# A soft mixture-of-experts stage: four places for the dispatch weights, its slot matrix loaded by block, and a later place for the second chunk's matmuls

## The chip, the cores and the metric

The kernel runs on one core of a Trainium2 chip. A core has a matrix engine (TensorE, PE in the profile; its weight loads are listed as PEld), a vector engine (VectorE, DVE), a scalar engine (ScalarE, ACT), a general engine (GpSimd, POOL) and a sync engine (SyncE, SP) that here issues the DMA transfers. Each engine works through its own queue of instructions in order and waits on semaphores where it needs another's result. The metric is the device time of one execution in microseconds (us).

## The reference

The reference is a sandwich of four layers on an input of 16 batch elements, 256 tokens and 128 features in float32. Every one of its eight sublayers computes `x = x + layernorm(sub(layernorm(x)))`: attention and a gated feed-forward in layer 0, linear and local attention and a soft mixture of experts in layer 1, attention and a feed-forward in layer 2, a state-space and attention trunk and an expert-choice mixture in layer 3. The change touches only the soft mixture of layer 1:

```python
def _L1_ffn_ref(x, phi, W, b):
    ...
    logits = jnp.einsum('bmd,dnp->bmnp', x, phi)
    dispatch = jax.nn.softmax(logits, axis=0)
    bsz, m, n, p = logits.shape
    combine = jax.nn.softmax(logits.reshape(bsz, m, n * p), axis=-1).reshape(bsz, m, n, p)
    slots = jnp.einsum('bmd,bmnp->bnpd', x, dispatch)
    y = jnp.einsum('bnpd,nde->bnpe', slots, W) + b[None, :, None, :]
    out = jnp.einsum('bnpd,bmnp->bmd', y, combine)
    return out
```

There are 64 experts (`n`) of 32 slots (`p`), so 2048 slots. The logits are normalised twice: over the 16 batch elements (`dispatch`, which mixes tokens into slots) and over the 2048 slots (`combine`, which mixes the experts' outputs back into tokens).

## The kernel before

One program computes all sublayers one after the other. The soft mixture is `stage_soft_moe` (line 1040). It works through the 2048 slots in 8 blocks of 256; a block has two chunks of 128 slots (4 experts each), and the 256 tokens are two tiles `t` of 128. The softmax over all slots is done with a running maximum: a block's outputs are added to `x` after the sum so far is faded by `exp(old maximum - new maximum)`.

Three generators do a block's work, and one iteration `n` of the loop at the end of the function runs them step by step side by side, for three blocks at once. Where a generator yields, the next one takes its step, so the source order of the steps is the order of priority; a scheduler then places the instructions into the engines' queues by that and by their dependences.

- `logits(n + 2)`: for each of the 16 batch elements two matmuls of the tokens with the block's 256 columns of `phi` into a PSUM bank `ps_s` (PE), a copy into `lg` (ScalarE, L1095) and a maximum into `mpart` (VectorE, L1096). Behind the last one come the running maximum `mtop` (L1100), its fade `mfade` (L1102, L1103) and `mless` (L1106).
- `slots(n + 1)`: `maxima(c, t)` for chunk c and tile t takes the maximum over the batch (VectorE, L1117 to L1120), subtracts it (L1121) and takes the exponential (ScalarE, L1122) in a tile `mdisp` of 8 KB per partition; `weights(c, t)` sums over the batch, takes the reciprocal and multiplies (VectorE, L1127 to L1134). `inputs(c, half)` multiplies tokens by these weights (PE, `ps_mm<-mdisp,mxn`) and ScalarE copies the result into `slT` (L1146); it needs both tiles' weights of the chunk. `experts(c, half)` adds the bias and multiplies by the expert's matrix `mw` (PE), and ScalarE copies into `my` (L1166). The expert matrices are loaded at the start of `slots` by SP.
- `share(n)`: for each batch element ScalarE takes the exponential of the logits (L1215), PE transposes it (`ps_t`, L1220), ScalarE copies the transpose into `meT` (L1222), PE multiplies with `my` (`ps_o`), VectorE adds into `x` (L1231; L1233 in the first block) and ScalarE takes the row sum into `mgot` (L1234). All its matmuls need the block's `my`, which is one buffer.

In the last block `share` starts an `end(g)` after every second batch element: the division by the sum of weights (L1249 to L1252), and for six of the eight groups a load of the stage's input back from DRAM into a tile of the name `slT` (SP, L1023) and the closing layer norm on VectorE and POOL (`soft_end`, up to L1037).

A tile name with a number of buffers is a ring of places: the next tile of that name waits until the readers of the oldest are done. `mdisp` has three places, `slT` three, `mw` two. PSUM is eight banks: two each for `mm`, `s`, `o` and `t`. `phi` is loaded whole (1024 KB) by one DMA near the program's start, with the stage's other weights, into a pool on the right side of the memory that is closed after this stage; work tiles lie on the left side. Behind the stage the program opens pools for the weights of layer 3 (`l_afc` and so on, `l3rows`) and starts layer 2's attention (`stage_l2_attn`), which begins with loads of its mask tables (`att_sel`, `att_rows`) through the same SP queue, casts of them on VectorE (`at_sel` L373, `b_rows` L375), and the reductions `at_nm` (L459).

Of the kernel before, what the change touches and what calls it, by code (L numbers as in the profile page):

```python
# [21 lines left out]
F32 = mybir.dt.float32  # L22
# [7 lines left out]
NB, SEQ, P, D = 16, 256, 128, 128  # L30
NG, NT, GT = 8, 4, 512
# [154 lines left out]
def idle(n):  # L186

    for _ in range(n):
        yield


def bc(ap, axis, n):

    ap = ap.unsqueeze(axis)
    shape = list(ap.shape)
    shape[axis] = n
    return ap.to_broadcast(shape)
# [842 lines left out]
def stage_soft_moe(k, x, w, wdram, bdram, xn, xs, fill):  # L1040
# [3 lines left out]

    nc, v = k.nc, k.nc.vector
    ident = k.c["ident"]
    phi = w["phi"]
    blocks, bs = 8, 2 * P
    sums = k.t([P, 2, NB], "sums", 1)
    xT = {}  # L1050
    tile_of = lambda b, t: (b // 2, 2 * (b % 2) + t)
# [3 lines left out]
    y = k.t([P, 2, NB, D + 1], "my", 1)  # L1055
# [4 lines left out]
    quarter = k.t([P, P], "mquarter", 1, dt=BF16)  # L1060
# [3 lines left out]
    def biases():  # L1064


        left = k.t([P, 16 * D], "mdisp", 3)
        nc.gpsimd.memset(left, 0.0)
        for i in range(3):
            nc.sync.dma_start(out=left[32 * i : 32 * i + 4, :], in_=bdram)  # L1070
        nc.gpsimd.tensor_copy(bias, left)
        for i in (1, 2):
            for at in (slice(32, 64), slice(64, P))[i - 1 :]:
                nc.gpsimd.tensor_tensor(left[at, :], left[at, :], bias[at, :], ALU.subtract)
                nc.gpsimd.tensor_copy(bias[at, :], left[at, :])

    def late(g):

        y = k.t([P, NT, D], "slT", 3)
        yield from k.norm_to(y, xn[g])  # L1080
        nc.gpsimd.tensor_tensor(x[g], x[g], y, ALU.add)
        yield
        yield from fill(g)

    def logits(n):
        lg = lgs[n % 2]
        part = k.t([P, 2, NB], "mpart", 2)
        for b in range(NB):
            if n == 0 and b % 2 == 0:
                xT[b // 2] = k.transposed(xn[b // 2], f"mxT{b // 2}", 1)  # L1090
            ps = k.ps("s").rearrange("p (t n) -> p t n", t=2)
            for t in range(2):
                g, at = tile_of(b, t)
                k.mm(ps[:, t, :], xT[g][:, at * P : (at + 1) * P], phi[:, n * bs : (n + 1) * bs])
            nc.scalar.copy(lg[:, :, b, :], ps)  # L1095
            v.tensor_reduce(part[:, :, b], ps, AX.X, ALU.max)  # L1096
            yield

        new = k.t([P, 2, NB], "mtop", 4)
        v.tensor_tensor(new, top[-1], part, ALU.max)  # L1100
        f = fade[n] = k.t([P, 2, NB], "mfade", 3)
        v.tensor_tensor(f, top[-1], new, ALU.subtract)  # L1102
        nc.scalar.activation(f, f, AF.Exp)  # L1103
        top.append(new)
        less[n] = k.t([P, 2, NB], "mless", 3)
        v.tensor_scalar(less[n], new, -1.0, None, ALU.mult)  # L1106

    def slots(n):

        lg = lgs[n % 2]  # L1110
        disp, rest = {}, []

        def maxima(c, t):
            src = lg[:, t, :, c * P : (c + 1) * P]
            e = disp[c, t] = k.t([P, NB, P], "mdisp", 3)
            m = k.t([P, P], "mm", 1)
            v.tensor_tensor(e[:, 0:8, :], src[:, 0:8, :], src[:, 8:16, :], ALU.max)  # L1117
            v.tensor_tensor(e[:, 0:4, :], e[:, 0:4, :], e[:, 4:8, :], ALU.max)
            v.tensor_tensor(e[:, 0:2, :], e[:, 0:2, :], e[:, 2:4, :], ALU.max)
            v.tensor_tensor(m, e[:, 0, :], e[:, 1, :], ALU.max)  # L1120
            v.tensor_tensor(e, src, bc(m, 1, NB), ALU.subtract)  # L1121
            nc.scalar.activation(e, e, AF.Exp)  # L1122

        def weights(c, t):
            e = disp[c, t]
            s = k.t([P, 4, P], "msum", 1)
            v.tensor_tensor(s, e[:, 0:4, :], e[:, 4:8, :], ALU.add)  # L1127
            for i in (8, 12):
                v.tensor_tensor(s, s, e[:, i : i + 4, :], ALU.add)
            for i in (2, 1):  # L1130
                v.tensor_tensor(s[:, 0:i, :], s[:, 0:i, :], s[:, i : 2 * i, :], ALU.add)
            r = k.t([P, P], "mrec", 1)
            v.reciprocal(r, s[:, 0, :])
            v.tensor_tensor(e, e, bc(r, 1, NB), ALU.mult)  # L1134

        def inputs(c, half):

            out = k.t([P, 8, P], "slT", 3)
            for q in range(2):
                ps = k.ps("mm").rearrange("p (b n) -> p b n", b=4)  # L1140
                for i in range(4):
                    b = 8 * half + 4 * q + i
                    for t in range(2):
                        g, at = tile_of(b, t)
                        k.mm(ps[:, i, :], xn[g][:, at, :], disp[c, t][:, b, :], t == 0, t == 1)
                nc.scalar.copy(out[:, 4 * q : 4 * q + 4, :], ps)  # L1146
            return out

        def experts(c, half, slT):

            pss = [k.ps("mm") for _ in range(2)]
            at = (2 * n + c) * D
            for ps in pss:
                k.mm(ps, quarter, bc(bias[:, at : at + D], 1, 4), True, False)
            for q, ps in enumerate(pss):
                for i in range(4):
                    for e in range(4):
                        k.mm(
                            ps[32 * e : 32 * e + 32, i * P : (i + 1) * P],
                            slT[:, 4 * q + i, 32 * e : 32 * e + 32],  # L1160
                            wc[c][:, e, :],
                            False,
                            True,
                        )
                b = 8 * half + 4 * q
                nc.scalar.copy(y[:, c, b : b + 4, 0:D], ps.rearrange("p (b n) -> p b n", b=4))  # L1166

        wc = []
        for c in range(2):
            at = 2 * n + c  # L1170
            wc.append(k.t([P, 4, D], "mw", 2))
            nc.sync.dma_start(out=wc[c].rearrange("p n d -> p (n d)"), in_=wdram[:, at * 512 : (at + 1) * 512])
        maxima(0, 0)
        yield
        maxima(0, 1)
        yield
        weights(0, 0)
        yield
        maxima(1, 0)
        yield  # L1180
        weights(0, 1)
        yield
        yield
        yield
        a = inputs(0, 0)
        yield
        b = inputs(0, 1)
        yield
        weights(1, 0)
        yield  # L1190
        maxima(1, 1)
        yield
        experts(0, 0, a)
        yield
        weights(1, 1)
        yield
        yield
        a = inputs(1, 0)
        yield
        experts(1, 0, a)  # L1200
        yield
        experts(0, 1, b)
        yield
        b = inputs(1, 1)
        yield
        experts(1, 1, b)

# [36 lines left out]
    def end(g, f, got):  # L1244


        bs = slice(2 * g, 2 * g + 2)
        r = k.t([P, 2, 2], "mend", 3)
        v.tensor_tensor(r, sums[:, :, bs], f[:, :, bs], ALU.mult)  # L1249
        v.tensor_tensor(r, r, got[:, :, bs], ALU.add)  # L1250
        rt = k.over[g] if g in k.over else k.t([P, NT], "mendt", 3)
        v.reciprocal(rt.rearrange("p (b t) -> p t b", b=2), r)  # L1252
        if g in k.over:
            return
        back = k.t([P, NT, D], "slT", 3)
        yield from soft_end(k, x[g], xs[:, g], rt, back)
        yield
        if g == 0:
            k.stats_nb(x[g], k.kept)
# [694 lines left out]
def program(ctx: ExitStack, tc: tile.TileContext, xin, dram, at, out):  # L1954
    nc = tc.nc
# [4 lines left out]
    def opened(name, side):  # L1960
        weights[name] = pool(name, side)
        return weights[name].__enter__()
# [4 lines left out]
    def load(p, name, only=None, dt=F32):  # L1967

        got = {}
        for n, (a, width) in at[name].items():  # L1970
            if only is not None and n not in only:
                continue
            src = dram[name][:, a : a + width]
            t = p.tile([src.shape[0], width], dt, tag=f"{name}_{n}", name=f"{name}_{n}")
            nc.sync.dma_start(out=t, in_=src)
            got[n] = t
        return got
# [20 lines left out]
    k = Ctx(tc, const, None, None)  # L1998
# [26 lines left out]
    closed("w0")  # L2025
    l2 = load(opened("wb", "right"), "l2")
    psoft = opened("soft", "right")
    l1f = load(psoft, "l1f")
    xs, xn, fill = soft_inputs(k, x, psoft)
    stage("l1a", "left", stage_l1_attn, l1, rows1, z, fill, xn, *hand, banks=RING_BANKS)  # L2030
    closed("z")
    closed("wa")

    stage("l1f", "left", stage_soft_moe, l1f, dram["l1fw"], dram["l1fb"], xn, xs, fill)
    closed("soft")
    pe = opened("we", "right")
# [50 lines left out]
```

## Time and profile before

Three runs took 2938.27, 2942.89 and 2943.25 us; their median is 2942.89.

| | us |
|---|---|
| median of three runs | 2942.89 |
| the profiled execution | 2940.6 |
| span of its profile | 2938.8 |
| the soft mixture in it | 931 to 1516.5 |
| mean granted clock of PE | 0.973 |

The profile is that of one execution. Its page begins with the busy time of each engine over the whole span; the trace behind it answers for any stretch of time. Four views are used below. The table by windows gives the busy time of each engine in a stretch. The timeline lists the instructions of one engine in order: start in us from the span's start, duration in us, engine, source line, operation, output tile, input tiles, shape, how many stand in the row, and in square brackets how long the engine had sat idle before it and on which engine's result it had waited. The DMA view gives size and time from issue to landing of each transfer, and the list of waits sums the idle times. Work on PE is listed at L336 whatever it computes, since a helper issues it, so its rows are told apart by their tiles.

Some rows of the stage, in us from the start of one instruction to the start of the next on the same engine:

| work | engine | us |
|---|---|---|
| logits of a batch element, 2 matmuls | PE | 0.86 |
| transposes of a batch element, 4 | PE | 0.44 |
| outputs of a batch element, 4 matmuls | PE | 0.89 |
| `inputs(c, half)` | PE | 3.57 |
| `experts(c, half)` | PE | 2.84 |
| maxima of a chunk and tile | VectorE | 4.46 |
| weights of a chunk and tile | VectorE | 5.4 |
| exponential of `mdisp` | ScalarE | 1.92 |
| copy of a 512-wide PSUM bank | ScalarE | 0.5 |
| `mpart` | VectorE | 0.60 |

### The profile page before, as it was taken

The page shows a single profiled execution, that of the slowest core. Times are in us where ns is not written, and L with a number is a line of the kernel's source. Part 1 is how long each engine was busy: PE and PEld are TensorE (multiplying, and loading weights), DVE is VectorE, ACT ScalarE, POOL GpSimd, SP SyncE. Part 2 cuts the span into 40 slices and gives each one's busy share as a digit, 9 for nine tenths or more (in the row PEclk, how much of TensorE's full clock was granted, in tenths as well). Part 3 has the DMA queues.
Part 4 walks back from the last instruction along what each step waited for, and adds up shares of the span by engine and source line. Part 5 has one row for each costly group of instructions (what it writes and reads, how often), then busy time and mean ns, then how long its engine had stood idle before and what let it go on. Part 6 is the DMA issues. An engine that isn't in the chain of part 4 may idle for free.

```text
span 2938.8 us, 59589 instructions
## 1 busy us (share of the span) xinstructions
PE 2729.7 (93%) x23673; PEld 1845.0 (63%) x23674; DVE 1953.3 (66%) x5309; ACT 1717.5 (58%) x3568; POOL 1017.2 (35%) x1406
## 2 busy tenths in 40 slices
PE   8889999999998799999978998899999799989998
PEld 4556667766666588888853443566666444436897
DVE  5665666666675989999866765666574677736542
ACT  6756566666665567777735665444444277756443
POOL 3543333333345100000044555422231466545332
PEclk9999999999999899999988999899999899999999
DMA  4000000000000000000020000000000000010000
GB/s 117 12 1 1 2 1 2 2 2 2 5 12 24 1 16 9 8 9 8 9 71 5 1 1 1 1 1 1 1 1 1 2 1 1 1 33 27 2 16 16
DMA packets 29150, 31.30 MB, mean 11 GB/s; under 512 B 7292, under 2 KB 20156, under 8 KB 28732
## 3 DMA queue, kind: packets, MB, share of 16 engines
q1 hardware_dynamic: 28872, 27.49, 3.1%
q8 instruction: 187, 3.06, 0.4%
q14 instruction: 91, 0.75, 0.1%
HBM read 23.29 MB, written 4.19 MB: 9 GB/s over the span
## 4 chain that ended last, share of the span: by engine, by line
PE 69%; ACT 12%; DVE 11%; POOL 5%; issue 2%; DMA 0%; POOLq 0%; SPq 0%; ACTq 0%; DVEq 0%
PE ps_s L336 44%; PE ps_o L336 10%; PE ps_mm L336 6%; PE ps_s L325 3%; ACT e L949 2%; ACT at_e L491 1%; POOL ln_rs L245 1%; ACT lg L1215 1%; DVE xn L264 1%; PE ps_xin L336 1%; ACT meT L1222 1%; POOL e L952 1%; PE ps_sum L336 1%; ACT L949 1%; ACT mdisp L1122 1%
## 5 line engine op out<-in xcount | busy, mean ns | idle before, releaser
L459 DVE TENSOR_REDUCE at_nm<-ps_s 128x2 f32<-128x512 f32 (+1 forms) x384 | 238.1, 682 | 119.6 <-PE ps_s L336 119.6
L491 ACT ACTIVATE at_e<-ps_s 128x512 f32<-128x512 f32 x384 | 198.2, 604 | 97.0 <-PE ps_s L336 94.8
L1504 DVE TENSOR_TENSOR scan<-ps_s,lm 128x384 f32<-128x384 f32 x256 | 124.7, 549 | 142.4 <-PE ps_s L336 142.1
L497 POOL TENSOR_SCALAR_AFFINE_SELECT at_e<-at_e 128x1024 f32<-128x1024 f32 (+1 forms) x96 | 135.1, 1407 | 209.0 <-ACT at_e L491 208.7
L245 POOL TENSOR_TENSOR ln_rs<-ln_rs,mhalf 128x4 f32<-128x4 f32 x192 | 196.1, 1021 | 15.8
L1031 POOL TENSOR_TENSOR ln_rs<-ln_mv,mendt 128x4 f32<-128x4 f32 x6 | 1.2, 200 | 521.0 <-DVE ln_mv L1029 521.0
L244 POOL TENSOR_SCALAR ln_rs<-ln_mv 128x4 f32<-128x4 f32 x184 | 39.6, 215 | 371.2 <-DVE ln_mv L257 352.8
L336 PE MATMUL ps_o<-my,meT 128*128 128x129 f32 x1024 | 142.5, 286 | 22.2 <-ACT mgot L1234 18.4
L336 PE MATMUL ps_s<-l1f_phi,mxT 128*128 128x256 f32 x512 | 141.6, 401 | 21.6 <-DVE mpart L1096 15.9
L899 DVE TENSOR_REDUCE l_max<-ps_s 128x3 f32<-128x384 f32 x256 | 124.8, 551 | 51.4 <-PE ps_s L336 49.1
L952 POOL TENSOR_SCALAR_AFFINE_SELECT e<-e 128x512 f32<-128x512 f32 x128 | 78.9, 637 | 217.2 <-ACT e L949 217.2
L336 PEld LDWEIGHTS ps_o<-my,meT 128*128 128x128 f32 x1024 | 126.3, 193 | 40.5 <-ACT mgot L1234 24.1
L336 PE MATMUL ps_s<-qm,kT 32*128 32x512 f32 x768 | 144.0, 652 | 8.0 <-DVE at_nm L459 7.8
L336 PE MATMUL ps_s<-km,qT 32*128 32x512 f32 x768 | 138.2, 667 | 11.3 <-DVE qT L1648 3.7
L336 PEld LDWEIGHTS ps_o<-l_w,mlp_h 128*128 128x128 f32 x1024 | 126.0, 192 | 19.1 <-issue 12.8
L336 PE MATMUL ps_o<-at_e,at_vm 128*32 128x128 f32 (+1 forms) x2048 | 123.2, 338 | 15.3 <-ACT at_oT L521 15.3
L336 PE MATMUL ps_o<-l_w,mlp_h 128*128 128x128 f32 x1024 | 130.1, 276 | 4.0 <-ACT oT L969 3.9
L336 PE MATMUL ps_s<-b_negmask,b_ident 128*128 128x256 bf16 (+1 forms) x640 | 123.6, 303 | 8.1 <-DVE b_negmask L780 1.4
L1481 ACT COPY BT<-ps_s 128x512 f32<-128x512 f32 x64 | 37.5, 587 | 158.1 <-PE ps_s L336 158.1
L336 PE MATMUL ps_mm<-mdisp,mxn 128*128 128x128 f32 x1024 | 125.3, 279 | 5.0 <-DVE mdisp L1134 4.9
L336 PEld LDWEIGHTS ps_mm<-mdisp,mxn 128*128 128x128 f32 x1024 | 121.8, 195 | 7.9 <-DVE mdisp L1134 6.6
L336 PE MATMUL ps_s<-xT,l_w 128*128 128x512 f32 x256 | 124.4, 607 | 1.3 <-ACT xT L811 1.3
(469 smaller groups left out, 7192.5 us busy)
## 6 DMA issues: line engine op xcount, KB each, us to landing
mw<-in_l1fw SPq DMA_DIRECT2D x16, 256.0 KB, 2.6
moe_w<-in_moe SPq DMA_DIRECT2D x16, 256.0 KB, 5.3
l_w<-in_l SPq DMA_DIRECT2D x10, 256.0 KB, 3.3
x<-in_x SPq DMA_DIRECT2D x8, 256.0 KB, 5.1
xs<-x SPq DMA_DIRECT2D x8, 256.0 KB, 2.1
out<-x SPq DMA_DIRECT2D x8, 256.0 KB, 2.3
slT<-xs SPq DMA_DIRECT2D x6, 256.0 KB, 2.8
l1f_phi<-in_l1f SPq DMA_DIRECT2D x1, 1024.0 KB, 5.0
```

The source lines that it names most:

```text
L244: g.tensor_scalar(out, in_, scale, eps, ALU.mult, ALU.add)
L245: g.tensor_tensor(out, out, self.mhalf[:, :n], ALU.pow)
L325: self.nc.tensor.transpose(out[:n, k * P : (k + 1) * P], src[:, k, cols], self.c["ident"])
L336: self.nc.tensor.matmul(out, lhsT=lhsT, rhs=rhs, start=start, stop=stop, skip_group_check=True)
L459: v_.tensor_reduce(nm[:, t, r, vs], s, AX.X, ALU.max, negate=True)
L491: nc.scalar.activation(e[:, r], s, AF.Exp)
L497: nc.gpsimd.affine_select(at, at, [[0, 4], [0, n], [1, P]], ALU.is_ge, 0.0, base=0, channel_multiplier=-1)
L899: v.tensor_reduce(mx[:, b, :, h, 16], s, AX.X, ALU.max, negate=True)
L949: nc.scalar.activation(e[:, h].rearrange("p j n -> p (j n)"), s[:, : 3 * P], AF.Exp)
L952: nc.gpsimd.affine_select(e[:, :, j, :], e[:, :, j, :], [[0, 4], [1, P]], ALU.is_ge, 0.0, base=0, channel_multiplier=-1)
L1481: nc.scalar.copy(s, ps)
L1504: v.tensor_tensor(m, s[:, : SEQ + P], lm[:, SCAN_HEADS[4 * (t // 2) + 2 * i + hh], :], ALU.mult)
```

## The change

The tile `mdisp` gets a fourth place; `slT` goes from three places to two. `phi` isn't loaded whole any more: its first 256 columns are loaded at the start into `phi0`, and each block's `logits` begins with a DMA of the next block's 256 columns (128 KB) into a tile `mphi` with two places. In `slots` the maxima of the second chunk's second tile move from behind the second chunk's first weights to behind the first chunk's second weights. Behind the last weights stand four idle steps, and then the second chunk's inputs and the experts: `inputs(1, 0)` with `experts(0, 1)` in one step, `inputs(1, 1)`, `experts(1, 0)`, `experts(1, 1)`, where before the order was `inputs(1, 0)`, `experts(1, 0)`, `experts(0, 1)`, `inputs(1, 1)`, `experts(1, 1)`. `idle(4)` is an existing helper that yields four times.

```diff
-    phi = w["phi"]
     blocks, bs = 8, 2 * P
+    phis = [w["phi0"]]
...
-        left = k.t([P, 16 * D], "mdisp", 3)
+        left = k.t([P, 16 * D], "mdisp", 4)
...
-        y = k.t([P, NT, D], "slT", 3)
+        y = k.t([P, NT, D], "slT", 2)
...
         lg = lgs[n % 2]
+        phi = phis[n]
+        if n + 1 < blocks:
+            phis.append(k.t([P, bs], "mphi", 2))
+            nc.sync.dma_start(out=phis[-1], in_=w["phi"][:, (n + 1) * bs : (n + 2) * bs])
...
-                k.mm(ps[:, t, :], xT[g][:, at * P : (at + 1) * P], phi[:, n * bs : (n + 1) * bs])
+                k.mm(ps[:, t, :], xT[g][:, at * P : (at + 1) * P], phi)
...
-            e = disp[c, t] = k.t([P, NB, P], "mdisp", 3)
+            e = disp[c, t] = k.t([P, NB, P], "mdisp", 4)
...
-            out = k.t([P, 8, P], "slT", 3)
+            out = k.t([P, 8, P], "slT", 2)
...
         weights(0, 1)
         yield
+        maxima(1, 1)
         yield
         yield
         a = inputs(0, 0)
...
         weights(1, 0)
         yield
-        maxima(1, 1)
-        yield
         experts(0, 0, a)
         yield
+        yield
         weights(1, 1)
-        yield
-        yield
+        yield from idle(4)
         a = inputs(1, 0)
+        experts(0, 1, b)
+        yield
+        b = inputs(1, 1)
         yield
         experts(1, 0, a)
-        yield
-        experts(0, 1, b)
-        yield
-        b = inputs(1, 1)
         yield
         experts(1, 1, b)
...
-        back = k.t([P, NT, D], "slT", 3)
+        back = k.t([P, NT, D], "slT", 2)
...
-    l1f = load(psoft, "l1f")
+    l1f = load(psoft, "l1f", {"quarter"})
+    a, width = at["l1f"]["phi"]
+    l1f["phi"] = dram["l1f"][:, a : a + width]
+    l1f["phi0"] = psoft.tile([P, 2 * P], F32, tag="phi0", name="phi0")
+    nc.sync.dma_start(out=l1f["phi0"], in_=l1f["phi"][:, : 2 * P])
```

More of the change, by code (lines that the diff above doesn't have):

```diff
@@ L1190, in slots @@
         yield
-        maxima(1, 1)
-        yield
         experts(0, 0, a)
         yield
+        yield
         weights(1, 1)
-        yield
-        yield
+        yield from idle(4)
         a = inputs(1, 0)
-        yield
-        experts(1, 0, a)
-        yield
         experts(0, 1, b)
@@ L1204, in slots @@
         b = inputs(1, 1)
+        yield
+        experts(1, 0, a)
         yield
```

## The prediction

> **What bounds the kernel now.** The change lies inside one of the sublayers, the soft mixture (931 to 1516.5 us of the span), so I read the page only for the engines' shares and then that stage by itself. The shares first: no engine but PE could set the whole, and what it did the table by windows must say. I cut the stage at the instruction that folds a block's last logits into the running maxima (`mtop`, L1100: 1012.5, 1083.6, then every 65.2 us up to 1410.1); two full blocks and the last one with the ending:
>
> ```profile
> PE 2729.7 (93%) x23673; PEld 1845.0 (63%) x23674; DVE 1953.3 (66%) x5309; ACT 1717.5 (58%) x3568; POOL 1017.2 (35%) x1406
> ```
> ```profile
> 1213.12:1278.35 65.23, 63.03 (x650) 55.15 (x649) 59.66 (x101) 47.60 (x102) 0.00 (x0) 1.00 0.03 10
> 1278.35:1343.59 65.24, 63.04 (x651) 55.16 (x650) 59.66 (x101) 47.59 (x102) 0.00 (x0) 1.00 0.03 9
> 1408.83:1464.89 56.06, 50.50 (x589) 44.10 (x588) 50.19 (x86) 39.33 (x86) 0.00 (x0) 1.00 0.04 11
> 1464.89:1516.50 51.61, 38.34 (x423) 33.16 (x422) 28.64 (x137) 17.17 (x44) 20.09 (x42) 0.92 0.30 95
> ```
>
> Columns after the length: busy PE, PE weight load, VectorE (DVE), ScalarE (ACT), POOL, granted clock, DMA share, GB/s. In a block PE is idle for 2.2 us of 65.2 and VectorE for 5.6: both are nearly full, so neither alone is the bound; they hand small waits to each other. Third, the timeline of VectorE and PE in one block tells which waits:
>
> ```profile
> 1220.41 0.69 DVE L1127 TENSOR_TENSOR msum<-mdisp 128x512 f32<-128x512 f32 x1 [1.98 <-ACT mdisp L1122]
> 1221.36 0.60 DVE L1231 SCALAR_TENSOR_TENSOR x<-x,mfade,ps_o 128x128 f32<-128x128 f32 x2 [0.25 <-PE ps_o L336]
> ...
> 1237.96 0.69 DVE L1127 TENSOR_TENSOR msum<-mdisp 128x512 f32<-128x512 f32 x1 [0.42 <-ACT mgot L1234]
> ```
> ```profile
> 1242.53 1.92 ACT L1122 ACTIVATE mdisp<-mdisp 128x2048 f32<-128x2048 f32 x1
> 1244.34 0.15 ACT L1234 COPY mgot<-ps_o 128x2 f32<-128x2 f32 x1
> ```
> ```profile
> 1244.55 1.72 PE L336 MATMUL ps_o<-my,meT 128*128 128x129 f32 x13 [1.21 <-ACT mgot L1234]
> ```
>
> VectorE waits for ScalarE's exponential of the first dispatch weights with nothing to put between: the next maxima (L1117, at 1227.30) need a `mdisp` place, and there are three; the place comes free when PE's inputs end at 1225.16. And one 1.92 us exponential ahead of a small eviction (`mgot`) has already stopped PE's outputs for 1.21 us. Last, the stage's two ends:
>
> ```profile
> 1024.77 0.69 DVE L1127 TENSOR_TENSOR msum<-mdisp 128x512 f32<-128x512 f32 x1 [1.98 <-ACT mdisp L1122]
> ...
> 1033.45 2.36 DVE L1117 TENSOR_TENSOR mdisp<-lg 128x1024 f32<-128x1024 f32 x2 [2.44 <-PE ps_mm L336]
> ```
> ```profile
> 1480.03 0.61 DVE L1231 SCALAR_TENSOR_TENSOR x<-x,mfade,ps_o 128x128 f32<-128x128 f32 x2 [14.60 <-PE ps_o L336]
> ```
>
> In the first blocks VectorE loses 0.78 (1009.52), 1.98 and 2.44; in the last one it waits 14.60 us while PE works off inputs and experts before the last outputs can start. There PE's tail counts, not VectorE.
>
> **The change part by part.** No arithmetic is added or removed; PE's work per block, from the starts of one row to the next, stays logits 13.8, transposes 7.0, outputs 14.2, inputs 14.3, experts 10.4 = 59.7 us; VectorE's is 59.7 too.
>
> *Fourth `mdisp` place and the earlier third maxima.* In the new order of instructions VectorE starts the next block's first two maxima before any wait, and the third follows inside the first weights. That covers 1.98 + 0.25 + 0.42 = 2.65 us a block, if VectorE sets the end. Late next is PE. On ScalarE the exponential of the third maxima (1.92) now stands ahead of the first `mgot` eviction, a logits eviction and the second `meT` copy, all of which PE waits for. Following the four queues by hand with the rows' durations, PE stops 1.85 us before the second batch element's outputs, 0.65 and 0.70 before two later ones: 3.2 us, against 0.29 + 1.21 + 0.29 + 0.41 = 2.2 now. By PE's waits alone a block takes 65.2 + 1.0 = 66.2; by VectorE's alone 65.2 − 2.65 = 62.6. Following the queues to the next `mtop` I get 64.3 to 65; I take 64.9 (−0.33), nearer the PE end since PE has less room. Five periods: **−1.7**.
>
> *The late inputs and experts.* `idle(4)` moves the inputs of the second chunk, and the experts but one, behind the last logits: 2 × 3.57 and 3 × 2.84 = 15.7 us of PE stand between the last logits and the next outputs. Before, 15 us stood there too (1211.55 to 1228.00 with 1.4 us of outputs and logits between), since those steps slipped behind; the edit mostly writes down what was happening. But the next block's transposes, which were done early, now partly wait for the last experts: +0.2 to +1.5, inside the 64.9.
>
> *Front.* The first block's `mtop(1)` moves from 1012.5 to about 1017, as 5 to 7 logits now stand behind the second weights (PE loses nothing: that stretch is VectorE's, with weights and maxima of 4.46 + 5.4 us each). In exchange the 71.1 us to the next `mtop` loses its wait of 2.44 and most of 1.98: 1017 + 64.9 = 1081.9 against 1083.6: **−1.7**; ends −5 (all of 0.78 + 1.98 + 2.44) and +1.
>
> *Ending.* VectorE's chain is shorter by 3 to 5 us, but it waits 14.60 there. PE's tail before the last outputs keeps its length, and two transposes come behind the last experts (4 × 0.11 each, plus their evictions, 1.5). From the last `mtop` to the first of the last outputs I find 69 us in both orders: **0**, ends −3 and +1.5. The six closing chains run at 5.7 us pitch from there, unchanged.
>
> *Phi by block.* Before: one 1024 KB load at 40 us, landing in 5.0. After: 128 KB at the start and seven of 128 KB, each issued at a block's first logits for the block after. The row of 256 KB at 2.6 us and that of 1024 at 5.0 give 3.1 ns per KB, so some 2.2 us each, 17.6 in sum. Here a rule of the Trainium skill speaks against the change: "DMA: Bandwidth & Descriptors", under Bandwidth, says to batch to at least 1 MiB; its table has 0.95 us for 64 KB and 6.15 for 1 MB, which by size gives about 1.4 for 128 KB, 11 in sum. So in transfer time the edit costs 12.6 by the rows or 5 by the page's figures. I take neither: each load has a block of 65 us to land in, and the DMA share in a block is 0.03. Cost **0**; had it to be waited for, 2.2 us times seven, 15. The added issues stand on SP ahead of `mw` loads (0.43 each), which are asked for a block ahead as well.
>
> *Two `slT` places.* The closing loads into `slT` and the experts' inputs now alternate over two; a place is free when POOL's sum two elements back is done, 11 us (two pitches) before it is needed, and a load lands in 2.8. **0**, to +1.
>
> *Loads of a later stage.* With phi gone the pools lie differently, and the new order of waits shows that the weights of the last layer (`l_afc` to `l3rows`), which go at 1476 to 1491 while the stage ends, wait for its end. They are 256 KB loads at 230 to 269 GB/s by the windows, some 11 to 15 us; behind them in SP's queue stand `att_sel` and `att_rows`, which the next stage (attention) casts on VectorE, before at 1518.37 and 1519.70, and a `back` load that is used only from 1548 on. I expect them about 12 us after the stage's end, when VectorE comes to them at 12.4 after eight reductions of 0.61: cost **+0.75**, ends 0 and +3 (its masks need `b_rows`; PE has 1 to 2 us of scores queued).
>
> Sum: −1.7 − 1.7 + 0 + 0 + 0.75 = −2.65. On the profiled execution's 2940.6 us (span 2938.8) that is 2937.9; the median of the three runs shown is 2.3 above it, so I give 2942.9 − 2.65 = 2940. This is within 0.2% (5.9 us), about what a measurement of this kernel can tell from no change.
>
> **The rivals.** *Faster: VectorE sets the block.* Then 1.9 of the 2.65 comes through each time (the 0.42 and a part of the 0.25 are already PE's): −9.5 in five periods, −5 in front, +0.75: 2929. For it: the inputs and experts stand in one piece, so that PE's new waits could fall where it is ahead anyway; against: PE is busy for 63 of 65.2.
>
> *Slower: ScalarE's exponential stands in the outputs' way.* The place is the second batch element's outputs; price 3.2 us for 2.2 saved at best, so +1.0 a block, and nothing of VectorE's gain comes through: +5 in five periods, +0.5 in front, +1.5 in the ending, +3 for the late loads: 2953. It decides from the point where PE's waits grow above the 2.2 us of today while VectorE still reaches the last logits with time to spare. For it: the row of 1.21 at 1244.55.
>
> *The change does little it says:* three places were short only for some 2 us a block, and the moved inputs were late already; then only the loads' shift is left: 2943 to 2946. It falls into my own case.
>
> **How the numbers follow.** My case with that last one 0.38, the slower 0.33, the faster 0.26, others (a later stage meets the late loads more hardly, or a changed order in the front) 0.03. The likeliest case alone is 2934 to 2947. The range takes in most of both others: 2927 to 2956. My case gives 0.32 to same, 0.05 to faster and 0.01 to slower; the slower one lies above +5.9 with all but 0.02; so faster 0.31, same 0.35, slower 0.34.
>
> **What would show it.** Right: `mtop` at about 1017, then a pitch of 64.3 to 65; no wait of L1127 for L1122 over 1 us; PE waiting for `mgot` some 1.8 us once a block; stage end within 3 us of 1513; `at_sel` cast some 12 us after it. Wrong: a pitch under 63.5 (VectorE was the bound) or over 66 (ScalarE's order), or a gap on PE in the attention stage behind `b_rows`.

## The result and the profile after

The changed kernel takes 2933.16 us (median of ten runs, 2930.93 to 2939.47), the kernel before beside it 2942.53 (ten runs). The ratio is 0.9971, with a 95% interval of 0.9962 to 0.9981: faster by 0.3%, which is clear of no change but small. The profiled execution has a span of 2929.9 us, 8.9 less than before. Its table by windows, cut at the running maximum (L1104 now; the windows before were cut 1.3 us ahead of it, which changes no length): two full blocks, the last one and the ending. Columns after the length as before: busy PE, weight load, VectorE, ScalarE, POOL, clock, DMA share, GB/s.

```profile
1204.26:1269.65 65.39, 64.29 (x665) 56.31 (x664) 60.86 (x104) 47.75 (x103) 0.00 (x0) 1.00 0.04 12
1269.65:1330.71 61.06, 60.72 (x636) 53.04 (x635) 58.14 (x100) 45.88 (x99) 0.00 (x0) 1.00 0.04 10
1396.11:1451.07 54.96, 50.49 (x574) 45.22 (x573) 48.81 (x85) 38.63 (x84) 0.00 (x0) 0.94 0.04 11
1451.07:1503.60 52.53, 39.47 (x442) 34.00 (x440) 28.23 (x135) 16.66 (x42) 20.12 (x41) 0.95 0.13 41
```

Blocks now come in pairs of 65.39 and 61.06: the scheduler alternates between two orders, and the place of the mark moves with them. Only the mean over a pair, 63.2, is a pitch; it was 65.2. PE is idle 1.4 us in two blocks, before 4.4; VectorE 7.5, before 11.2. So PE, nearly full now, sets the pitch. The last block has a clock of 0.94, where before it had 1.00.

VectorE's timeline at the place of the old 1.98 us wait. The wait is gone, since the block's second maxima (L1126 at 1211.64, the subtraction in `maxima(0, 1)`) now fill the time of the first exponential:

```profile
1209.00 2.28 DVE L1126 TENSOR_TENSOR mdisp<-lg,mm 128x2048 f32<-128x2048 f32 x1
1211.20 0.18 DVE L1244 TENSOR_TENSOR sums<-sums,mfade 128x32 f32<-128x32 f32 x1
1211.32 0.29 DVE L1125 TENSOR_TENSOR mm<-mdisp 128x128 f32<-128x128 f32 x1
1211.64 2.29 DVE L1126 TENSOR_TENSOR mdisp<-lg,mm 128x2048 f32<-128x2048 f32 x1
1213.92 0.69 DVE L1132 TENSOR_TENSOR msum<-mdisp 128x512 f32<-128x512 f32 x1
```

ScalarE's and PE's timelines where the third exponential (that of `maxima(1, 0)`) now stands ahead of small evictions. It is there as foreseen, but PE has logits and transposes to do meanwhile and waits 0.80 us:

```profile
1220.87 1.91 ACT L1127 ACTIVATE mdisp<-mdisp 128x2048 f32<-128x2048 f32 x1 [0.44 <-DVE mdisp L1126]
1222.68 0.14 ACT L1237 COPY mgot<-ps_o 128x2 f32<-128x2 f32 x1
1222.72 0.59 ACT L1099 COPY lg<-ps_s 128x512 f32<-128x512 f32 x1
1223.20 0.60 ACT L1225 COPY meT<-ps_t 128x512 f32<-128x512 f32 x1
```
```profile
1223.85 1.16 PE L336 MATMUL ps_o<-my,meT 128*128 128x129 f32 x8 [0.80 <-ACT meT L1225]
```

In the other order of the pair the exponential comes behind the copies, and PE does not wait for it at all. Its only wait in that block is one of 0.29 us, elsewhere:

```profile
1285.65 0.59 ACT L1225 COPY meT<-ps_t 128x512 f32<-128x512 f32 x1
1286.13 0.17 ACT L1237 COPY mgot<-ps_o 128x2 f32<-128x2 f32 x1
1286.18 1.93 ACT L1127 ACTIVATE mdisp<-mdisp 128x2048 f32<-128x2048 f32 x1
```
```profile
1303.47 0.66 PE L1223 MATMUL ps_t<-const_ident,lg 128*128 128x128 f32 x4 [0.29 <-ACT meT L1225]
```

The ending did not become shorter. VectorE's wait before the last outputs is now longer than the 14.60 us of before:

```profile
1467.91 0.61 DVE L1234 SCALAR_TENSOR_TENSOR x<-x,mfade,ps_o 128x128 f32<-128x128 f32 x2 [16.31 <-PE ps_o L336]
```

In the attention stage behind, the table's cast now waits for its load:

```profile
1517.51 0.17 DVE L373 COPY at_sel<-att_sel 128x4 f32<-128x4 f32 x1 [1.13 <-DMA att_sel<-in_att]
```

By stretches, against the profile before: start of the mixture to its first running maximum and all ahead of it −2.5; from there to the third −2.2; five pitches −9.3; from the last running maximum to the stage's end **+1.7**; everything behind **+3.4**. Sum −8.9. So 14 us came in, 11.5 of them behind the first running maximum, and 5 were given back, and the question is which part of the change did which. (The first running maximum lies between 961.6 and 969.8 us in the kernels below, with no order that follows their edits; it is counted for none of them.)

### The profile page after: what moved, and what is told of

It is laid out like the page before. It is cut to its first block, busy times and chain, and to the rows that moved or that the text cites. A ratio compares the mean times of both kernels' runs of the same rounds, so it can differ in the third digit from the quotient of the medians.

```text
span 2929.9 us, 59646 instructions
## 1 busy us (share of the span) xinstructions
PE 2727.9 (93%) x23674; PEld 1842.9 (63%) x23674; DVE 1949.6 (67%) x5309; ACT 1713.0 (58%) x3568; POOL 1017.7 (35%) x1406
## 4 chain that ended last, share of the span: by engine, by line
PE 71%; ACT 11%; DVE 11%; POOL 5%; issue 2%; DMA 0%; SPq 0%; POOLq 0%; ACTq 0%; DVEq 0%
PE ps_s L336 44%; PE ps_o L336 11%; PE ps_mm L336 7%; PE ps_s L325 3%; ACT e L949 2%; POOL ln_rs L245 1%; ACT at_e L491 1%; PE ps_t L1223 1%; DVE xn L264 1%; PE ps_xin L336 1%; POOL e L952 1%; PE ps_sum L336 1%; ACT L949 1%; ACT lg L1218 1%; DVE l_max L899 1%
## 5 line engine op out<-in xcount | busy, mean ns | idle before, releaser
L336 PE MATMUL ps_mm<-mdisp,mxn 128*128 128x128 f32 x1024 | 129.6, 284 | 10.5 <-DVE mdisp L1139 10.4
L336 PE MATMUL ps_s<-mphi,mxT 128*128 128x256 f32 x448 | 123.2, 395 | 14.2 <-DVE mpart L1100 13.9
L336 PEld LDWEIGHTS <-b_ident 128*128 128x128 bf16 x656 | 57.2, 99 | 109.2 <-issue 91.3
```

The source lines that it names most:

```text
L336: self.nc.tensor.matmul(out, lhsT=lhsT, rhs=rhs, start=start, stop=stop, skip_group_check=True)
```

## Experiments

The table has every profiled kernel by its own trace, one execution each. T0, T2 and T7 are the first, third and last running maximum, S the end of the stage (the end of the last `over` reciprocal). The ratio is the time against runs of the kernel before that were made beside it (4 to 13 runs of each kernel, 10 to 24 of the kernel before).

| kernel | ratio (95%) | T0 to T2 | pitch T2 to T7 | T7 to S | T0 to S | S to end |
|---|---|---|---|---|---|---|
| before | | 119.5 | 65.29 | 106.2 | 552.2 | 1422.5 |
| changed | 0.9971 (0.9962–0.9981) | 117.4 | 63.42 | 107.9 | 542.4 | 1425.9 |
| phi | 1.0008 (0.9997–1.0019) | 119.5 | 65.29 | 106.3 | 552.2 | 1423.1 |
| res | 0.9950 (0.9933–0.9967) | 114.3 | 63.27 | 101.9 | 532.5 | 1425.1 |
| order3 | 0.9977 (0.9969–0.9985) | 116.0 | 65.33 | 105.3 | 548.0 | 1422.0 |
| latemax | 0.9949 (0.9934–0.9964) | 114.6 | 63.56 | 101.7 | 534.1 | 1425.4 |
| earlymax | 0.9993 (0.9984–1.0001) | 120.4 | 64.84 | 105.7 | 550.3 | 1426.0 |
| late7 | 0.9940 (0.9927–0.9953) | 117.2 | 63.43 | 101.7 | 536.1 | 1424.9 |
| resatt | 0.9933 (0.9917–0.9948) | 114.4 | 63.25 | 101.8 | 532.5 | 1423.4 |
| lateatt | 0.9930 (0.9915–0.9944) | 112.6 | 63.50 | 101.7 | 531.8 | 1423.4 |

How far a single profile can be trusted shows in kernels with the same steps in a stretch. Their pitches agree within 0.1 us. From T0 to T2, before and phi, res and resatt, changed and late7 agree within 0.2 us, but latemax and lateatt differ by 2.0.

**The place or the order?** Kernel res has the changed kernel's tiles and loads with the step order of before:

```diff
         weights(0, 1)
         yield
-        maxima(1, 1)
         yield
         yield
...
         weights(1, 0)
         yield
+        maxima(1, 1)
+        yield
         experts(0, 0, a)
         yield
-        yield
         weights(1, 1)
-        yield from idle(4)
+        yield
+        yield
         a = inputs(1, 0)
-        experts(0, 1, b)
-        yield
-        b = inputs(1, 1)
         yield
         experts(1, 0, a)
         yield
+        experts(0, 1, b)
+        yield
+        b = inputs(1, 1)
+        yield
         experts(1, 1, b)
```

> The changed kernel's tiles (four places for the dispatch weights, two for slT, phi by block) with the order of steps of before. Theory A, the place carries it: VectorE no longer waits for a place, so the pitch of the running maxima falls from 65.2 us to about 63.2 as in the changed kernel, and the time to about 2933 us. Theory B, the order of the steps carries it: the pitch stays within 0.5 us of 65.2, and the time is 2940 to 2946 us, with the loads of layer 3 late as in the changed kernel (+1).

Its pitch is 63.27 and its ratio 0.9950: theory A. Its stage is also 9.9 us shorter than that of the whole change (532.5 against 542.4); the intervals of the two ratios still touch. Kernel order3 is the counterpart, the new order with three places:

```diff
-        left = k.t([P, 16 * D], "mdisp", 4)
+        left = k.t([P, 16 * D], "mdisp", 3)
...
-            e = disp[c, t] = k.t([P, NB, P], "mdisp", 4)
+            e = disp[c, t] = k.t([P, NB, P], "mdisp", 3)
```

> The changed kernel with three places for the dispatch weights in place of four. Theory A (the place): the early third maxima of a block must wait for a place until the inputs of the first chunk's weights are read, VectorE stops for 2 us or more a block, pitch 65 us or more, time at or above 2940 us. Theory B (the order): pitch within 0.5 us of 63.2, time 2931 to 2935 us.

The pitch is back at 65.33, and VectorE's timeline has the old wait at the old place, of the same length:

```profile
1217.07 2.29 DVE L1126 TENSOR_TENSOR mdisp<-lg,mm 128x2048 f32<-128x2048 f32 x1
1221.34 0.69 DVE L1132 TENSOR_TENSOR msum<-mdisp 128x512 f32<-128x512 f32 x1 [1.98 <-ACT mdisp L1127]
```

The pitch is theory A's, though VectorE's stop is not where A put it. The expectation's "early third maxima" are the moved `maxima(1, 1)`, the fourth in source order. They do start late (1260.10, 46 us into the block, about where they stood before), but VectorE has other work until then; it is the next block's second maxima that leave it idle, as before. The ratio is 0.9977, a little better than A said: 3.5 us come in between T0 and T2, the stretch in which single profiles differ by up to 2.0. With res and order3 together, the 2 us a block belong to the fourth place: 65.3 to 63.3 in the old order, 65.3 to 63.4 in the new. One kernel was left between them: does phi by block bring something itself? Kernel phi is the kernel before with phi by block and nothing else (three places for `mdisp`, three for `slT`).

> The kernel before with phi loaded by block and nothing else: three places for the dispatch weights, three for slT, the old order. Theory A (the fourth place alone carries the gain): pitch stays at 65.2 us within 0.2, the stage is as long as before, and only the late loads of layer 3 cost up to 1 us: ratio 0.999 to 1.002, 2942 to 2950 us beside the kernel before. Rival: loading phi by block brings a part itself (less memory traffic or earlier start of the stage): pitch under 64.7 or the stage shorter by over 3 us.

It brings nothing: 552.2 us of stage in both, the pitch equal to the hundredth. What it does, by the tile sizes, is make room: the whole `phi` takes 8 KB a partition, `phi0` and two `mphi` 3 KB, so with the 4 KB of the third `slT` place there are 9 KB for the 8 KB of the fourth `mdisp` place. No kernel has four places beside the whole `phi`, and none changes the `slT` places alone.

**What do the two reorderings do?** Kernel latemax moves the second chunk's second maxima back behind `weights(1, 0)` and keeps the late inputs; kernel earlymax keeps the early maxima and puts inputs and experts back.

```diff
         weights(0, 1)
         yield
-        maxima(1, 1)
         yield
         yield
...
         weights(1, 0)
         yield
+        maxima(1, 1)
+        yield
         experts(0, 0, a)
```

> The changed kernel with the second chunk's second maxima at the step of before; the late inputs and experts stay. Theory B1, the late inputs and experts carry the gain (PE's outputs no longer wait behind evictions): pitch stays at 63 to 63.5 us, time 2931 to 2935. Theory B2, the early maxima carry it: pitch 64.5 us or more, time 2938 or more.

```diff
         weights(1, 0)
         yield
-        experts(0, 0, a)
         yield
+        experts(0, 0, a)
         yield
         weights(1, 1)
-        yield from idle(4)
+        yield
+        yield
         a = inputs(1, 0)
-        experts(0, 1, b)
-        yield
-        b = inputs(1, 1)
         yield
         experts(1, 0, a)
         yield
+        experts(0, 1, b)
+        yield
+        b = inputs(1, 1)
+        yield
         experts(1, 1, b)
```

> The changed kernel with the inputs and experts at the steps of before; the second chunk's second maxima stay early, with four places. Theory B1 (late inputs and experts carry it): pitch 64.5 us or more, time 2938 or more. Theory B2 (early maxima with four places carry it): pitch 63 to 63.5 us, time 2931 to 2935.

Both theories asked which of the two *carries* the gain, and both were beside the point. The early maxima alone take most of the fourth place's gain away (64.84 against 63.27 in res); the late inputs alone cost little (63.56); the two together come back to 63.42. The pitch of latemax is close to what B1 foresaw, and earlymax is as B1 foresaw too, but res shows that nothing is carried by either: in the full blocks the late inputs only repair what the early maxima break. Where earlymax loses it shows on PE. In every full block of it PE stops for 1.01 us behind an exponential of ScalarE that stands ahead of the `meT` copy, then for 0.56 behind another copy and for 0.85 behind VectorE's weights: 2.4 us, about as much as the 2.2 before the change. VectorE stands 4.28 us before a logits maximum in every block, and so has time to spare. Why the early maxima leave ScalarE and VectorE in this order was not followed further.

```profile
1241.73 1.91 ACT L1127 ACTIVATE mdisp<-mdisp 128x2048 f32<-128x2048 f32 x1
1243.59 0.60 ACT L1227 COPY meT<-ps_t 128x512 f32<-128x512 f32 x1
```
```profile
1244.24 1.16 PE L336 MATMUL ps_o<-my,meT 128*128 128x129 f32 x8 [1.01 <-ACT meT L1227]
1250.62 4.06 PE L336 MATMUL ps_mm<-mdisp,mxn 128*128 128x128 f32 x34 [0.85 <-DVE mdisp L1139]
```
```profile
1279.73 0.69 DVE L1100 TENSOR_REDUCE mpart<-ps_s 128x2 f32<-128x512 f32 x1 [4.28 <-ACT lg L1099]
```

**Why is the changed kernel's ending 6 us longer than that of latemax?** Its trace gives a candidate in the last block. VectorE subtracts the early maxima of `maxima(1, 1)` (L1126 at 1423.36) ahead of the multiplication of the weights that PE needs (L1139 at 1425.50). No logits are left by then that PE could do meanwhile, and it waits; after that 28 matmuls take 6.21 us (28 like them took 3.29 at 1449.98). VectorE, PE, and three windows there:

```profile
1423.36 2.23 DVE L1126 TENSOR_TENSOR mdisp<-lg,mm 128x2048 f32<-128x2048 f32 x1
1425.50 2.28 DVE L1139 TENSOR_TENSOR mdisp<-mdisp,mrec 128x2048 f32<-128x2048 f32 x1
```
```profile
1424.35 0.66 PE L1223 MATMUL ps_t<-const_ident,lg 128*128 128x128 f32 x4 [0.29 <-ACT meT L1225]
1427.83 6.21 PE L336 MATMUL ps_mm<-mdisp,mxn 128*128 128x128 f32 x28 [2.83 <-DVE mdisp L1139]
```
```profile
1423.53:1426.94 3.41, 1.19 (x9) 0.71 (x7) 3.41 (x2) 2.08 (x3) 0.00 (x0) 1.00 0.00 0
1426.94:1433.77 6.83, 5.94 (x28) 5.94 (x29) 6.62 (x12) 5.96 (x16) 0.00 (x0) 0.50 0.00 0
1433.77:1437.18 3.41, 3.41 (x32) 3.41 (x32) 3.33 (x6) 3.10 (x7) 0.00 (x0) 1.00 0.02 5
```

In the kernel before the same inputs waited 0.36 us and ran at full clock:

```profile
1440.83 3.39 PE L336 MATMUL ps_mm<-mdisp,mxn 128*128 128x128 f32 x28 [0.36 <-DVE mdisp L1134]
```

Kernel late7 takes the maxima back in the last block alone:

```diff
-        maxima(1, 1)
+        if n < blocks - 1:
+            maxima(1, 1)
         yield
...
         weights(1, 0)
         yield
+        if n == blocks - 1:
+            maxima(1, 1)
+            yield
         experts(0, 0, a)
```

> The changed kernel with the second chunk's second maxima at their old place in the last block alone. Theory: in the last block the early maxima (2.23 us of VectorE for the subtraction) stand ahead of the weights that PE waits for, PE idles 2.8 us and its clock falls to half for about 5 us: without that the time from the last running maximum to the stage's end falls from 107.9 to about 102 us, the clock of that stretch is 1.00, the pitch of the earlier blocks stays at 63.4, and the ratio is about 0.995. Rival: the longer ending is that of the late inputs and experts (PE's tail before the last outputs): it stays at 106 to 108 us, ratio 0.997.

The theory holds: 101.7 us, the other stretches of the stage as they were, and the same inputs follow the transposes without a wait and at full clock. Here is PE's timeline of late7, and its window from T7 to the last outputs:

```profile
1428.50 0.66 PE L1227 MATMUL ps_t<-const_ident,lg 128*128 128x128 f32 x4 [0.29 <-ACT meT L1229]
1429.06 6.96 PE L336 MATMUL ps_mm<-mdisp,mxn 128*128 128x128 f32 x60
```
```profile
1398.91:1464.64 65.73, 63.96 (x836) 55.76 (x835) 49.01 (x88) 44.31 (x95) 0.00 (x0) 1.00 0.08 22
```

60 matmuls take 6.96 us there, against 6.21 for 28. Of the 6.2 us (107.9 − 101.7), 2.8 are the wait and 2.9 the slow matmuls (6.21 − 3.29); the last 0.5 was not traced.

**What does the attention stage lose?** Kernels resatt and lateatt are res and latemax with the two tables loaded near the program's start into a pool that stays:

```diff
     rows1 = load_rows(base, "l1rows")
+    k.att = load(base, "att")
...
-        with self.tc.tile_pool(name="att", bufs=1) as pool:
-            got = self.load(pool, "att")
+        got = self.att
```

> The changed kernel's tiles with the order of steps of before, and the attention's two tables loaded near the program's start, so that they do not stand behind the weights of layer 3. Theory, the late tables are what the attention stage lost (1.67 us of VectorE's wait and what follows): the time after the stage's end falls from 1425.1 to 1422 to 1424 us, ratio 0.994 to 0.9945. Rival, what the later part lost is a granted clock that differs from run to run: it stays within 0.5 us of 1425, ratio 0.995.

> The changed kernel with the second chunk's second maxima at their old place in all blocks, and the attention's two tables loaded near the program's start. By the theory of the late tables 1 to 2 us under the same kernel without it (ratio 0.9949 there): 0.9943 to 0.9947; by the rival 0.9949. Pitch 63.6 as without it.

The casts wait for no load now:

```profile
1502.56 1.73 DVE L372 COPY at_sel<-att_sel 128x4 f32<-128x4 f32 x1 [0.29 <-DVE over L1256]
```

What stands behind the stage takes 1423.4 us in both, 1.7 and 2.0 less than without (1425.1 and 1425.4), within the range foreseen for resatt. But this difference is not the delay of the tables. It shows when the same reduction `at_nm` is looked up in both traces, in us behind S:

| reduction | res | resatt | latemax | lateatt |
|---|---|---|---|---|
| 9th | 17.46 | 15.89 | 17.14 | 15.89 |
| 41st | 64.98 | 65.31 | 64.70 | 65.30 |
| 81st | 122.51 | 122.84 | 122.24 | 122.83 |
| 97th | 150.62 | 149.38 | 150.35 | 149.37 |

The late tables cost res 1.6 us at first, and at the 41st reduction it has made them up. It falls back by 1.6 between the 81st and the 97th, and there its granted clock is 0.94 where that of resatt is 1.00. The windows of this stretch, res and then resatt:

```profile
1622.60:1650.71 28.11, 27.48 (x213) 11.93 (x212) 17.02 (x33) 17.02 (x39) 15.97 (x23) 0.94 0.01 1
```
```profile
1625.10:1651.65 26.55, 25.92 (x213) 11.61 (x212) 17.01 (x34) 17.01 (x39) 15.96 (x23) 1.00 0.01 2
```

So the lasting difference is one of granted clock, as the rival had it, and what the late tables cost is not shown. Nor is it shown that they play no part in the slow stretch: the four kernels whose `at_sel` cast waits for its load (changed, res, latemax, late7) have it and the two with early tables do not, but phi and earlymax, whose `b_rows` cast waits 0.72 and 1.14 us for a load, do not have it either, and each was profiled once. The changed kernel's +3.4 behind the stage is of the same kind: 0.3 at the 81st reduction, 1.8 at the 97th with a clock of 0.97 between 110 and 160 us behind S (1.00 before the change), and the rest later than the 191st, 284 us behind S.

The ratios, 0.9933 and 0.9930, have intervals that overlap with those of res and latemax. Both kernels are faster than the kernel before by 0.7%, and faster than the changed kernel. The four places do that with the order of steps as it was; whether the early tables add to it stays open.

## Why the prediction was right or wrong

The measured 2933 us lies between the likeliest case (2940, alone 2934 to 2947) and the faster rival (2929). The likeliest case, no change, was not what came: −2.65 us was summed, −8.9 measured in the profile, and the range held the result because it took in the rival. The faster rival had the size of the main term, 9.5 us for five pitches against 9.3. It was right that PE's new waits fall where PE is ahead anyway, but not that VectorE sets the block: in the changed kernel VectorE is idle for 7.5 us of two blocks and PE for 1.4.

- **Fourth place.** Right in what it removes: the 1.98 us wait is gone, and VectorE's idle time in a block fell from 5.6 to 3.7 us, as much as the pitch (1.9). The step that failed is the price set against it: "PE stops 1.85 us before the second batch element's outputs, 0.65 and 0.70 before two later ones: 3.2 us". Measured are 0.80 in one block and 0.29 in the next, 0.55 a block. I had followed one order of the queues and taken it for all blocks; the schedule alternates between two, and in one of them the exponential stands behind the copies PE needs. That is only a part of the error: in the order that was followed PE stops for 0.80 and not for 3.2. With 0.55 for 3.2, PE's end of the bounds would have been 65.2 − 2.2 + 0.55 = 63.6, and the value taken could not have been 64.9.
- **PE's work in a block.** Four experts of 2.84 us are 11.4 and not 10.4, so the rows sum to 60.7 us and not to 59.7. No later step of the prediction uses this sum.
- **Late inputs and experts.** Said to write down what was happening already; by latemax against res they cost 0.3 us a pitch, by lateatt against resatt as much. Over the whole stage the two pairs differ (+1.6 and −0.7), by the stretch from T0 to T2. Right in kind.
- **Front.** The second running maximum was foreseen at about 1017 and came at 1017.8, which is luck: in this profile the first one came 2.5 us earlier than before (961.6 against 964.1), so the stretch between them was 56.2 us where 1017 − 964.1 = 52.9 was meant. The stretch to the third was 61.2 and not 64.9, the side on which the fourth place was mis-sized too. The two errors nearly cancel: 117.4 us in all, and 117.8 meant.
- **Ending.** Foreseen 0, measured +1.7, above the upper bound of +1.5 by little, but for another reason. Without the early maxima the ending is 4.5 us shorter than before (101.7 against 106.2), more than the gain of 3 that was the lower bound. VectorE's chain was held not to matter, since "it waits 14.60 there"; but ahead of that wait PE waits for VectorE's weights, and by then no logits are left to put between.
- **Phi by block, two `slT` places.** Foreseen 0, measured 0 for phi (552.2 us both). A 128 KB load lands in 2.0 us, where 2.2 was worked out from the rows; the estimate of 1.4 was worked out from the figures of the Trainium skill ("DMA: Bandwidth & Descriptors", under Bandwidth; a straight line between its two gives 1.3). Its table is of loads issued by GpSimd and leaves out the issuing, so it does not measure the same as issue to landing on SP. The rows were nearer, and the eight loads cost nothing. With two `slT` places no wait for a closing load shows in the changed kernel's ending.
- **Late loads.** The `at_sel` cast was expected about 12 us after the stage's end and stood at 13.5, after a wait of 1.13. Foreseen +0.75 within 0 to 3. At the 9th reduction the changed kernel is 1.4 us later than before (17.24 against 15.80), at the 41st 0.3; what lasts of it is not shown.
- **The slower rival** named the right row (an exponential ahead of evictions) with too high a price. The early maxima did turn out to be the harmful part. In the last block it is VectorE's queue that stops PE; in the full blocks of earlymax an exponential ahead of a copy stops it for 1.01 us, as this rival said, and VectorE's weights for 0.85.

## What to carry to other kernels

When an engine waits with nothing to put between, first ask whether it is a place that is missing: here one more buffer gave the whole gain, and the reordering that came with it took a part of it back. Test the parts of such a change one by one, since two of them may only repair each other. Work moved ahead in a loop is free only as long as the waiting engine has something else to do, so look at the last iteration by itself. And before a difference of 1 or 2 us behind the change is put down to a cause, look up the same instruction in both traces at several places: here a delay of 1.6 us was made up within 65 us, and one of the same size came in later by the granted clock.

## What the runs showed of the hardware

In the changed kernel PE stands still from 1425.0 to 1427.8, the wait of 2.83 us. By the three windows above the clock was still full up to 1426.94 and then half for 6.83 us, 5.94 of them with PE at work. So it fell when the stop had lasted 1.9 us, and the half clock cost as much again as the wait (2.8 us of wait, 2.9 of slow matmuls). The Trainium skill ("TensorE: Matmul & The Clock Gate", in Part 1) puts the return to the slow state after at least one idle window of about 3.4 us. In this trace the 3.41 us ahead of the fall were not idle throughout: PE was busy for 1.19 of them, nearly all of it with eight transposes. No run here varies how busy such a stretch must be, nor whether transposes count in it. Before the change, a stretch in which PE was busy for 1.62 of 4 us at about the same place left the clock at 1.00:

```profile
1434.00:1438.00 4.00, 1.62 (x12) 1.39 (x13) 3.96 (x9) 3.07 (x7) 0.00 (x0) 1.00 0.00 0
```
